# The hybrid layer and its FP4 FFN as a fourth layer of the batch flow

## The chip, the cores and the metric

The kernel runs on one core of one Trainium2 chip. The metric is the device time of one execution in microseconds, taken as the median of several runs. The engines are named TensorE (PE, and PEld for its weight loads), VectorE (DVE), ScalarE (ACT), GpSimd (POOL) and SyncE (SP), which issues DMAs. Each works through its own instructions in order and waits on semaphores for the others.

## The reference

Eight sequences of 512 tokens with 128 features pass through sixteen residual layers, `x = x + f(layernorm(x))`: four groups of attention, FFN, another attention, FFN. The last two layers are the ones that are moved, `L3_attn_b` (called the hybrid here) and `L3_ffn`; the second is also the FFN of the layer before the hybrid.

```python
def hybrid(x):                              # b, s, d = 8, 512, 128
    xn = rms(x, w_norm_in)
    route_in = xn.mean(axis=1)
    probs = softmax(silu(route_in @ router_w1) @ router_w2 + router_b2)
    p_medium, p_full = probs[:, 1], probs[:, 2]
    ssm_out = scan(state = lam * state + (1 - lam) * xn)    # over the tokens
    a1 = softmax(q1 @ k1.T / sqrt(32)); a2 = softmax(q2 @ k2.T / sqrt(32))
    slr_out = ((a1 - slr_lam * a2) @ v) @ slr_wo
    mixed = ssm_out + (p_medium + p_full) * slr_out
    mixed[:, -1] += p_full * (softmax(xn[:, -1] @ landmarks.T / sqrt(d)) @ landmarks)
    out = x + rms(concat([mixed, xn]) @ mix_w, w_norm_out)
    summary = out.mean(axis=1) @ bus_compress               # one row per sequence
    return out + 0.1 * (summary @ bus_publish) @ bus_expand

def fp4_linear(x, w):                       # blocks of 16, E2M1 grid
    return fp4_quant_dequant(x) @ fp4_quant_dequant(w).T

def ffn(x):
    return fp4_linear(silu(fp4_linear(x, w_gate)) * fp4_linear(x, w_up), w_down)
```

The `ttt` branch of the original has no effect on its output and is left out above; with a single published row per sequence its softmax is 1.

## The kernel before

All of `x` stays on the chip as eight batches (the sequences, `xb(b)`) of four tiles of 128 tokens. The first eight layers run one after the other, each with its own order, and are not touched but for where their constants lie. Then comes the flow: `stream([l2a, l2b, l3a])` takes three attention layers, each with its FP4 FFN, as 24 virtual batches `v = 8 * layer + b`. The work of a virtual batch is cut into named steps: layer norm (`st`, `sh`, `ap`), projections (`T`, `pq` ... `rv`), running maxima of the scores (`m` with group, head and unit, reduced in `f`, placed by `h` and `i`), scores and exponentials (`x`), weighting (`w`, `c`, `t`, `d`), output (`aT`, `po`, `bi`, `o0` to `o4`, `ad`), the FFN's norm, quantising and transpose (`F0` to `F8`), gates and their Silu (`V`, `S`, line 1324), up product (`U`, `y`), quantising of the hidden quarter (`z`, `D`, `C`, `A`, `M`) and the narrow product (`n`, `N`, `E`).

`in_order` issues them: the string `STREAM` is one iteration, a word `name:k` takes the step of the batch that entered k iterations ago, and there are 24 + 5 = 29 iterations, 0 to 28. Nothing is scheduled behind that: the words' order is the order on every engine. The steps of the FFN proper stand at 5, so a batch's FFN runs five iterations after its norm. PSUM is two pairs of banks (`sc`) and four single banks (`bank`), shared by all steps. In `quantize_part` the rounding of quarters 0 and 2 of the hidden tile runs on VectorE and that of quarters 1 and 3 on GpSimd.

Behind the flow, `hybrid` (line 2228) loads its weights, first norms, transposes and sums all eight batches, runs one router for the eight at once, joins the bus matrices (lines 2333 to 2339), and then runs `hybrid_batches`, a software pipeline of its own over the batches: scores of 512 by 512 for two maps (line 2387), their maxima (2391), exponentials (2396), the difference of the two maps (2411 to 2415), a product with a scaled identity that transposes it (2425), copies (2426), the weighting (2437), the mix (2459, 2460) and the norm of the output. Behind that `fp4_ffn` runs the last FFN in a pipeline of its own (lines 2151 to 2179), with the quantising of a whole hidden tile of 1408 columns at a time (lines 1984 to 2012).

```python
for i in range(B + 4):
    b1, b2, b3, b4 = (k if 0 <= k < B else None for k in (i, i - 1, i - 2, i - 3))
```

Of the kernel before, what the change touches and what calls it, by code (L numbers as in the profile page):

```python
# [22 lines left out]
F32 = mybir.dt.float32  # L23
# [6 lines left out]
P = 128  # L30
# [3 lines left out]
FF = 352  # L34
# [48 lines left out]
class Net:  # L83
    def __init__(self, ctx, tc, a):
# [12 lines left out]
        xd = a["X"].rearrange("b (t p) d -> p (b t) d", p=P)  # L97
        nc.sync.dma_start(self.xb(0), xd[:, 0:NT, :])
        self.c = g.tile([P, N_CONST], F32, name="consts")
        nc.scalar.dma_start(self.c, a["consts"])  # L100
        for b in range(1, B):
            nc.sync.dma_start(self.xb(b), xd[:, b * NT : (b + 1) * NT, :])
# [4 lines left out]

        self.maskbf = g.tile([P, 2 * P], BF16, name="maskbf")
        for k in range(2):
            nc.vector.tensor_copy(self.maskbf[:, k * P : (k + 1) * P], self.cc(C_MASK + 384, P))  # L110
# [7 lines left out]
        nc.gpsimd.memset(self.least[:, 1:2], -1e-12)  # L118

# [10 lines left out]
    def cc(self, at, n):  # L130
        return self.c[:, at : at + n]
# [440 lines left out]
    def moe(self, side=None):  # L572
# [17 lines left out]
        with self.tc.tile_pool(name="moe", bufs=2) as pool, self.tc.tile_pool(  # L590
# [35 lines left out]
            else:  # L626
# [40 lines left out]
                le, bc(at[0:1], 1, TILES), bc(self.c[0:1, C_IOTA : C_IOTA + TILES], 2, EXPERTS), ALU.is_le  # L667
# [249 lines left out]
    def max_parts(self, pool, dram, qs, ks, head, causal):  # L917
# [8 lines left out]
        def unit(g, j, u):  # L926
            if not box:
                box["nm"] = pool.tile([P, NT, 16], F32, tag="nm", name="nm", bufs=3 if causal else 2)
                if causal:
                    box["pm"] = pool.tile([P, 16, 10], F32, tag="pm", name="pm", bufs=3)  # L930
# [177 lines left out]
    def stream(self, layers):  # L1108
# [5 lines left out]
        with tile_pool(name="flow_fix", bufs=1) as fix, tile_pool(name="flow", bufs=2) as pool, tile_pool(  # L1114
# [9 lines left out]
            def layer(n):  # L1124
                key, ffn_key, rope, eps, post = layers[n]
                w = self.weights(f"{key}_w")
                rows = self.rows(f"{key}_rows")
# [4 lines left out]
                if ffn_key not in ffn:  # L1132
                    ffn[ffn_key] = self.ffn_pool.tile([P, 2 * FF + 3 * P], F32, tag="fp4_w", name="fp4_w")
                    nc.scalar.dma_start(ffn[ffn_key], self.ffn[ffn_key])
# [158 lines left out]
            def ffn_parts(v, w, rows, cols, ffn_w, rope, eps, post):  # L1293

                b, box = v % B, {}
                gu, dn = ffn_w[:, 0 : 2 * FF], ffn_w[:, 2 * FF :].rearrange("p (c n) -> p c n", c=3)
# [69 lines left out]
            def parts(v):  # L1366
                n = v // B
                if n not in made:
                    made[n] = layer(n)
                loaded[v] = [None] * 4, [None] * 4, [None] * 4  # L1370
# [7 lines left out]
            self.in_order(self.STREAM, parts, B * len(layers))  # L1378
            self.sm = outer

# [6 lines left out]
        g0 f1:3 g1 S0:5 U0:5 x101:3 m120:2 U1:5 y0:5 w0:3 z0:5 y1:5 c0:3 D0:5 m132:2 m102:2 x111:3 h1:3 aT:4  # L1387
        t0:3 z1:5 d0:3 D1:5 C0:5 V1:5 A0:5 m100:2 i1:3 M0:5 S1:5 po:4 bi:4 C1:5 o0:4 m130:2 T:1 A1:5 m020:2
        U2:5 x112:3 y2:5 o1:4 m121:2 m002:2 n0:5 x102:3 pq:1 z2:5 o2:4 rq:1 Pq:1 D2:5 M1:5 mg x110:3 Rq:1
        o3:4 m112:2 U3:5 y3:5 m101:2 N0:5 E0:5 o4:4 ad:4 z3:5 D3:5 m131:2 x200:3 x201:3 m011:2 m021:2 w1:3  # L1390
        C2:5 A2:5 M2:5 F0:4 c1:3 x202:3 l3:2 m122:2 l2:2 x211:3 pk:1 rk:1 m001:2 x210:3 m010:2 n1:5 m031:2
        m022:2 x212:3 x311:3 C3:5 m012:2 m032:2 m000:2 m110:2 sq:1 Pk:1 m030:2 t1:3 m111:2 F1:4 A3:5 d1:3
        x310:3 n2:5 f0:2 Rk:1 w2:3 M3:5 F2:4 m302:2 m321:2 m331:2 N2:5 c2:3 h0:2 i0:2 x301:3 F3:4 N1:5 E2:5
        E1:5 F4:4 x302:3 m212:2 m202:2 m300:2 n3:5 sk:1 m200:2 m301:2 x300:3 m220:2 x312:3 N3:5 E3:5 m312:2
        m330:2 t2:3 m210:2 d2:3 pv:1 m201:2 m232:2 l1:1 rv:1 F5:4 x010:2 F6:4 F7:4 x000:2 st w3:3 x012:2
        c3:3 m322:2 m221:2 x011:2 m231:2 x100:2 m211:2 F8:4 t3:3 x002:2 d3:3 m310:2 sh x001:2 m222:2 m320:2
        V0:4 m332:2 l0:1 ap m230:2 m311:2
    """
    BLOCK = """
# [1326 lines left out]
```

## Time and profile before

| | |
| --- | --- |
| median of 3 runs | 3687.51 us (3686.36 to 3687.9) |
| profiled execution, its own time | 3658.49 us |
| its span, first to last instruction | 3656.8 us |
| granted TensorE clock, mean | 0.872 |
| TensorE, VectorE busy | 2905.8, 2488.8 us (79%, 68%) |
| ScalarE, GpSimd busy | 2001.4, 1797.9 us (55%, 49%) |
| chain that ended last | TensorE 50%, VectorE 17%, GpSimd 12%, DMA 9%, ScalarE 7% |

Times in the profile are counted from the span's start. Busy shares are means over stages with different limits, so the view by stretches says more: in the windows view each row is a stretch of time, with the busy microseconds of each engine, the number of its instructions in brackets, the granted clock, the share of the DMA engines and GB/s. The waits view names who waited, for whom, microseconds in total, times, and the longest. A row of a group of instructions ends in busy time and mean nanoseconds of one, then the idle time before them. A row of the timeline begins with start and duration in microseconds.

### The profile page before, as it was taken

What the parts mean: (1) busy time and instruction counts of PE and PEld (TensorE: products, weight loads), DVE (VectorE), ACT (ScalarE), POOL (GpSimd) and SP (SyncE); (2) the same over time, 40 slices, a digit from 0 to 9 for tenths busy, and PEclk for the clock granted to TensorE, in tenths of its full rate; (3) what the DMA queues carried; (4) which work ended last, traced back from release to release, by engine and by line L of the source; (5) the groups of instructions that cost most, each with busy time, mean ns of one, the idle gap of its engine ahead of it and who ended that gap; (6) DMA issues with size and microseconds to landing.
All of it is one profiled execution on the core that took longest, in us unless ns stands there. A gap on an engine that the chain in (4) does not pass through costs nothing.

```text
span 3656.8 us, 63518 instructions
## 1 busy us (share of the span) xinstructions
PE 2905.8 (79%) x21247; PEld 1888.6 (52%) x21247; DVE 2488.8 (68%) x6913; ACT 2001.4 (55%) x3877; POOL 1797.9 (49%) x2398
## 2 busy tenths in 40 slices
PE   4757928999958747585664899999999999976867
PEld 2436912333327735483564456666665666644546
DVE  4555328888744357543453799999999999965667
ACT  3432325777732333153333477888887777754444
POOL 2223443332014466244134478767787777763345
PEclk8877958999978967687877999999999999986778
DMA  2001232222001311021014222111121121100000
GB/s 92 10 16 40 67 95 68 64 64 67 29 14 52 102 28 29 15 56 29 24 45 107 80 73 68 71 68 66 63 76 62 60 73 59 63 8 1 1 1 24
DMA packets 129655, 185.56 MB, mean 51 GB/s; under 512 B 18994, under 2 KB 98354, under 8 KB 129206
## 3 DMA queue, kind: packets, MB, share of 16 engines
q1 hardware_dynamic: 99030, 134.88, 10.9%
q0 software_dynamic: 15616, 35.47, 3.8%
q10 hardware_dynamic: 14688, 11.14, 1.0%
q8 instruction: 176, 2.88, 0.3%
q14 instruction: 145, 1.19, 0.1%
HBM read 128.96 MB, written 52.46 MB: 50 GB/s over the span
## 4 chain that ended last, share of the span: by engine, by line
PE 50%; DVE 17%; POOL 12%; DMA 9%; ACT 7%; issue 3%; SPq 1%; DVEq 0%; ACTq 0%; POOLq 0%; PEld 0%; PEldq 0%
PE av L1054 6%; DMA k<-d 6%; PE sc L733 5%; PE av L749 5%; PE sc L1023 5%; PE mx L942 5%; PE m L244 2%; DVE nm L961 2%; ACT e L1033 2%; PE sc L1308 1%; PE mx L939 1%; POOL e L1036 1%; PE m L1153 1%; PE sc L386 1%; POOL got L800 1%
## 5 line engine op out<-in xcount | busy, mean ns | idle before, releaser
L1033 ACT ACTIVATE e<-sc 128x1024 f32<-128x1024 f32 (+1 forms) x832 | 742.5, 926 | 182.2 <-PE sc L1023 136.1
L954 DVE TENSOR_REDUCE pm<-mx 128x4 f32<-128x512 f32 (+1 forms) x1152 | 625.7, 593 | 45.2 <-PE mx L942 39.6
L942 PE MATMUL mx<-k,q 126*128 126x512 bf16 (+3 forms) x2048 | 545.4, 327 | 99.4 <-DMA k<-d 87.5
L1023 PE MATMUL sc<-q,k 128*128 128x512 bf16 (+3 forms) x2048 | 446.0, 321 | 14.2 <-ACT e L1033 12.9
L1036 POOL TENSOR_SCALAR_AFFINE_SELECT e<-e 128x256 f32<-128x256 f32 x768 | 296.6, 408 | 194.4 <-ACT e L1033 190.2
L961 DVE TENSOR_REDUCE nm<-mx 128x1 f32<-128x512 f32 x512 | 324.5, 684 | 84.7 <-PE mx L942 83.7
L712 POOL DMA_INDIRECT xg<-xd,srci x220 | 210.7, 958 | 344.7 <-DVE srci L705 191.9
L1054 PE MATMUL av<-e,vaug 128*32 128x512 f32 (+3 forms) x4096 | 370.0, 482 | 2.5 <-ACT e L1033 1.8
L942 PEld LDWEIGHTS <-q 126*128 126x128 bf16 x2048 | 198.0, 99 | 307.7 <-issue 237.8
L244 PE MATMUL m<-ident,xn 128*128 128x128 f32 x480 | 108.6, 335 | 256.2 <-ACT xn L212 117.9
L1023 PEld LDWEIGHTS <-k 128*128 128x128 bf16 x2048 | 179.7, 98 | 186.7 <-issue 107.6
L939 PE MATMUL mx<-maskbf,identbf 128*128 128x128 bf16 (+1 forms) x1152 | 262.7, 238 | 15.6 <-DVE h L1333 5.3
L733 PE MATMUL sc<-xgT,w1c 128*128 128x128 f32 x1760 | 240.8, 281 | 2.5 <-DVE w1c L721 2.5
L749 PE MATMUL av<-moe_w,h 128*128 x1760 | 234.7, 277 | 1.0 <-ACT xgT L727 0.6
L800 POOL DMA_INDIRECT got<-yd,posi x192 | 192.4, 1002 | 76.4 <-issue 49.9
L733 PEld LDWEIGHTS sc<-xgT,w1c 128*128 128x128 f32 x1760 | 222.6, 198 | 2.6 <-issue 2.6
L244 PEld LDWEIGHTS m<-ident,xn 128*128 128x128 f32 x480 | 68.1, 159 | 299.6 <-ACT xn L212 135.6
L749 PEld LDWEIGHTS av<-moe_w,h 128*128 128x128 f32 x1760 | 216.2, 194 | 2.0 <-ACT xgT L727 0.7
L1054 PEld LDWEIGHTS av<-e,vaug 128*32 128x32 f32 x4096 | 108.4, 110 | 192.8 <-issue 147.4
L233 ACT ACTIVATE xn<-x,ln_shift,rstd 128x128 f32<-128x128 f32 x352 | 144.7, 485 | 103.9 <-DVE ln_shift L228 103.8
L721 DVE COPY w1c<-moe_w 128x516 f32 x220 | 100.9, 459 | 136.3 <-DVE y L758 63.2
L736 ACT ACTIVATE h<-sc 128x512 f32<-128x512 f32 x142 | 84.8, 597 | 160.5 <-PE sc L733 160.2
(461 smaller groups left out, 6434.6 us busy)
## 6 DMA issues: line engine op xcount, KB each, us to landing
q<-d SPq DMA_DIRECT2D x128, 288.0 KB
k<-d SPq DMA_DIRECT2D x384, 96.0 KB
d<-thirds SPq DMA_DIRECT2D x48, 384.0 KB
yd<-y SPq DMA_DIRECT2D x220, 64.0 KB
xd<-xn ACTq DMA_DIRECT2D x24, 256.0 KB
d<-thirds SPq DMA_DIRECT2D x48, 128.0 KB
moe_w<-in_moe_w POOLq DMA_DIRECT2D x8, 516.0 KB
moe_w<-in_moe_w POOLq DMA_DIRECT2D x8, 512.0 KB
```

What stands on the lines that cost most here:

```text
L244: nc.tensor.transpose(pt[:, t * P : (t + 1) * P], src[:, t, :], self.ident)
L733: nc.tensor.matmul(ps[:, cols], lhsT=w1c[i][:, cols], rhs=xgT[i], start=True, stop=True)
L749: nc.tensor.matmul(ps[:, 0:P], lhsT=h[i][:, c * P : (c + 1) * P], rhs=w2[:, bass.ds(e + c * P, P)], start=c == 0, stop=c == 3,)
L800: nc.gpsimd.indirect_dma_start(got[b][k][:, i, :], None, yd, bass.IndirectOffsetOnAxis(ap=posi[:, j : j + 1], axis=0))
L939: nc.tensor.matmul(out, lhsT=self.identbf, rhs=mask, start=True, stop=False, skip_group_check=True)
L942: nc.tensor.matmul(s[:, col : col + n], lhsT=q[:, t, :], rhs=key[:, 0 : n // P, :], start=not causal, stop=True, skip_group_check=True,)
L954: nc.vector.tensor_reduce(box["pm"][:, h, at : at + n // P], s[:, 0:n].rearrange("p (k n) -> p k n", n=P), AX.X, ALU.max,)
L961: nc.vector.tensor_reduce(box["nm"][:, u, h : h + 1], s, AX.X, ALU.max, negate=True)
L1023: nc.tensor.matmul(s[:, jj, col : col + n], lhsT=key[:, t, :], rhs=q[:, at // P : (at + n) // P, :], start=True, stop=True,)
L1033: nc.scalar.activation(e, s[:, :, 0:wide], AF.Exp, scale=scale)
L1036: nc.gpsimd.affine_select(out=e[:, :, col : col + P], in_=e[:, :, col : col + P], pattern=[[0, 2], [1, P]], compare_op=ALU.is_ge, fill=0.0 ...
L1054: nc.tensor.matmul(acc[g][32 * j : 32 * j + 32, at : at + n], lhsT=vaug[:, t, first : first + 32], rhs=pair[j // 2][:, j % 2, col : col + ...
```

## The change

The hybrid becomes the fourth entry of the flow, `("l3b", "l3f", None, None, None)`, and `hybrid`, `hybrid_layer`, `hybrid_batches` and `fp4_ffn` are taken out. Its work is cut into steps `H` (norm, transpose, router, landmarks), `I` (queries, values, averages, scan), `K` with a tile (scores, maxima, exponentials, difference, transposing product, copy) and `J` (weighting, mix, norm, output, bus), with `st`, `sh`, `ap` in front and the flow's own FFN steps behind. The router runs for each batch by itself. The copies of the transposed weights are written in halves. `in_order` leaves one empty place (24) in front of the hybrid's batches, which take places 25 to 32. The weights of the hybrid take the slot of the first FP4 weights and are loaded by ScalarE's queue when the layer is first asked for, at the first word of iteration 25.

`STREAM` has 58 new words and its old words in a somewhat different order; `m320`, `m322` and `m311` go from 2 to 3. The tiles `nm` and `pm` have two buffers instead of three. The constants of the first layers move to a pool that ends before the flow, loaded in two pieces, with the rotary tables, which stay, as a third. Lines of code that are only moved or renamed are left out below, and of the hybrid's steps only some are shown.

```diff
+        nc, a = self.nc, self.a
+        xd = a["X"].rearrange("b (t p) d -> p (b t) d", p=P)
+        nc.sync.dma_start(self.xb(0), xd[:, 0:NT, :])
+        self.c = pool.tile([P, N_CONST - 2 * S], F32, name="consts")
+        nc.scalar.dma_start(self.c[:, 0:C_COS], a["consts"][:, 0:C_COS])
+        nc.scalar.dma_start(self.c[:, C_COS:], a["consts"][:, C_RSEL:])
+        for b in range(1, B):
+            nc.sync.dma_start(self.xb(b), xd[:, b * NT : (b + 1) * NT, :])
+        nc.scalar.dma_start(self.rotary, a["consts"][:, C_COS:C_RSEL])
...
+        if C_COS <= at < C_RSEL:
+            return self.rotary[:, at - C_COS : at - C_COS + n]
+        at -= 2 * S if at >= C_RSEL else 0
...
-                box["nm"] = pool.tile([P, NT, 16], F32, tag="nm", name="nm", bufs=3 if causal else 2)
+                box["nm"] = pool.tile([P, NT, 16], F32, tag="nm", name="nm")
                 if causal:
-                    box["pm"] = pool.tile([P, 16, 10], F32, tag="pm", name="pm", bufs=3)
+                    box["pm"] = pool.tile([P, 16, 10], F32, tag="pm", name="pm")
...
-                w = self.weights(f"{key}_w")
-                rows = self.rows(f"{key}_rows")
...
-                    ffn[ffn_key] = self.ffn_pool.tile([P, 2 * FF + 3 * P], F32, tag="fp4_w", name="fp4_w")
-                    nc.scalar.dma_start(ffn[ffn_key], self.ffn[ffn_key])
+                    ffn[ffn_key] = self.ffn_pool.tile([P, 1188], F32, tag="fp4_w", name="fp4_w")
+                    nc.scalar.dma_start(ffn[ffn_key][:, 0 : 2 * FF + 3 * P], self.ffn[ffn_key])
+                if rope is None:
+                    return self.hybrid_weights(fix), self.rows("l3b_rows"), None, ffn[ffn_key], rope, eps, post
+                w = self.weights(f"{key}_w")
+                rows = self.rows(f"{key}_rows")
...
+                if layers[n][2] is None:
+                    out = self.hybrid_parts(pool, v % B, *made[n][0:2])
+                    out.update(ffn_parts(v, *made[n]))
+                    return out
...
+            late = B * [x[2] for x in layers].index(None) if None in [x[2] for x in layers] else None
+            self.in_order(self.STREAM, parts, B * len(layers), late)
...
+    def hybrid_weights(self, fix):
+        nc, a = self.nc, self.a
+        w = self.ffn_pool.tile([P, 1188], F32, tag="fp4_w", name="l3b_w")
+        nc.scalar.dma_start(w, a["l3b_w"])
+        lam = w[:, 928:929]
+        keep = fix.tile([P, 1], F32, tag="keep", name="keep")
+        nc.vector.tensor_scalar(keep, lam, -1.0, 1.0, ALU.mult, ALU.add)
+        bus = w[:, 736:864]
+        for part in (w[:, 608:736], w[:, 480:608]):
+            ps = self.bank("m")
+            nc.tensor.transpose(ps[:, 0:P], part, self.ident)
+            turned = fix.tile([P, P], F32, tag="turned", name="turned")
+            nc.scalar.copy(turned, ps[:, 0:P])
+            ps = self.bank("m")
+            nc.tensor.matmul(ps[:, 0:P], lhsT=turned, rhs=bus, start=True, stop=True)
+            bus = fix.tile([P, P], F32, tag="bus", name="bus", bufs=1)
+            nc.vector.tensor_copy(bus, ps[:, 0:P])
+        return w, keep, bus
...
+        def hidden():
+            hid = box["hid"] = small(1, "hhid")
+            nc.scalar.activation(hid[0:64], box["r"][0:64, 0:1], AF.Silu, scale=1.0 / S)
...
+        def exponentials():
+            t = box["lg"]
+            nc.scalar.activation(t[0:1, 0:3], t[0:1, 0:3], AF.Exp, bias=t[0:1, 4:5], accum_out=t[0:1, 5:6])
+            t = box["at"]
+            nc.scalar.activation(
+                t[0:1, 0:64], t[0:1, 0:64], AF.Exp, bias=t[0:1, 64:65], scale=D**-0.5, accum_out=t[0:1, 65:66]
+            )
...
+        def scores(t):
+            s = tiles["s", t] = self.sc()
+            for k in range(2):
+                r = slice(32 * k, 32 * k + 32)
+                nc.tensor.matmul(
+                    s[:, k, :], lhsT=box["q"][r, t * P : (t + 1) * P], rhs=box["k"][r, :], start=True, stop=True
+                )
...
+        def maxima(t):
+            nm = tiles["nm", t] = self.small([P, 2], "df_nm")
+            nc.vector.tensor_reduce(nm, tiles["s", t], AX.X, ALU.max, negate=True)
+            nc.vector.tensor_scalar(nm, nm, scale, None, ALU.mult)
...
+        def exps(t):
+            s, nm = tiles.pop(("s", t)), tiles.pop(("nm", t))
+            tot = tiles["tot", t] = self.small([P, 2], "df_tot")
+            e = tiles["e", t] = pool.tile([P, 2, S], F32, tag="e512", name="e", bufs=6)
+            for k in range(2):
+                nc.scalar.activation(
+                    e[:, k, :], s[:, k, :], AF.Exp, bias=nm[:, k : k + 1], scale=scale, accum_out=tot[:, k : k + 1]
+                )
...
+        def differ(t):
+            e, tot = tiles["e", t], tiles.pop(("tot", t))
+            inv = self.small([P, 2], "df_inv")
+            nc.vector.reciprocal(inv, tot)
+            nc.vector.scalar_tensor_tensor(inv[:, 1:2], inv[:, 1:2], rows[:, 259:260], tot[:, 0:1], ALU.mult, ALU.mult)
+            over = tiles["over", t] = small(P, "hover")
+            nc.gpsimd.tensor_scalar(over, self.ident, inv[:, 0:1], None, ALU.mult)
+            nc.vector.scalar_tensor_tensor(e[:, 1, :], e[:, 1, :], inv[:, 1:2], e[:, 0, :], ALU.mult, ALU.subtract)
+        def turn(t):
+            e, over = tiles.pop(("e", t)), tiles.pop(("over", t))
+            pt = tiles["pt", t] = self.bank("m")
+            for k in range(NT):
+                kk = slice(k * P, (k + 1) * P)
+                nc.tensor.matmul(pt[:, kk], lhsT=e[:, 1, kk], rhs=over, start=True, stop=True)
+        def turned(t):
+            if t == 0:
+                box["AT"] = [pool.tile([P, 2, S], F32, tag="e512", name="AT", bufs=6) for _ in range(2)]
+            pt = tiles.pop(("pt", t)).rearrange("p (k q) -> p k q", k=NT)
+            for i, part in enumerate(box["AT"]):
+                nc.scalar.activation(
+                    part[:, :, t * P : (t + 1) * P], pt[:, 2 * i : 2 * i + 2, :], AF.Copy, scale=-1.0
+                )
...
+        parts = {"st": stats, "sh": shift, "ap": apply}
+        names = "abcdefghijklmnopq"
+        first = (first_squares, first_norm, turn_x, sum_tokens, route, hidden, at_landmarks, logits, biased)
+        first += (exponentials, shares, spread, gates, recall, recalled)
+        parts.update({f"H{n}": f for n, f in zip(names, first)})
+        second = (queries, keep_queries, value_products, values, averages, scan)
+        parts.update({f"I{n}": f for n, f in zip(names, second)})
+        last = (weigh, context, project_out, gated, mix, last_squares, last_norm, residual, sums, keep_sums, add)
+        last += (publish, published)
+        parts.update({f"J{n}": f for n, f in zip(names, last)})
+        for n, f in zip(names, (scores, maxima, exps, differ, turn, turned)):
+            parts.update({f"K{n}{t}": lambda f=f, t=t: f(t) for t in range(NT)})
+        return parts
...
+        g0 m320:3 S0:5 Hn:3 m322:3 x101:3 m112:2 U0:5 Ke1:3 Jg:4 m311:3 Hj:2 Ho:3 Jh:4 f1:3 Id:2 y0:5 m120:2
+        Jk:4 w0:3 z0:5 U1:5 y1:5 D0:5 c0:3 aT:4 x111:3 h1:3 z1:5 Kc3:3 Hk:2 t0:3 C0:5 g1 d0:3 i1:3 Kd3:3
+        V1:5 Ke2:3 A0:5 S1:5 D1:5 m130:2 Ka0:2 M0:5 m102:2 po:4 bi:4 m132:2 T:1 Kf1:3 C1:5 o0:4 m121:2 A1:5
+        Ji:4 x112:3 Kb0:2 m020:2 U2:5 pq:1 o1:4 Jj:4 Kf2:3 y2:5 n0:5 z2:5 rq:1 mg x102:3 m002:2 D2:5 x110:3
+        Jl:4 o2:4 m110:2 M1:5 Jm:4 U3:5 l2:2 y3:5 m100:2 Pq:1 N0:5 Kc0:2 z3:5 o3:4 Ka2:2 o4:4 Kd0:2 ad:4
+        x201:3 Ke3:3 E0:5 m031:2 m011:2 Ka1:2 Ke0:2 x200:3 Rq:1 D3:5 m101:2 w1:3 C2:5 c1:3 A2:5 M2:5 x202:3
+        F0:4 l3:2 Kf3:3 Ha:1 x210:3 m032:2 Kf0:2 Ja:3 Hl:2 Kb2:2 C3:5 m012:2 m131:2 Jb:3 pk:1 rk:1 x211:3
+        m021:2 n1:5 m030:2 m010:2 x212:3 sq:1 m122:2 x311:3 m022:2 m111:2 A3:5 t1:3 Pk:1 d1:3 M3:5 m001:2
+        Hm:2 m000:2 n2:5 Rk:1 x310:3 F1:4 f0:2 w2:3 m302:2 m321:2 Jc:3 m331:2 N2:5 Kb1:2 Jd:3 F2:4 h0:2 c2:3
+        i0:2 x301:3 x302:3 N1:5 E2:5 F3:4 E1:5 If:2 Kc2:2 m330:2 m301:2 Kc1:2 Je:3 n3:5 F4:4 m200:2 Hb:1
+        m201:2 sk:1 Kd1:2 x312:3 m210:2 t2:3 N3:5 E3:5 Jf:3 Hc:1 d2:3 Hd:1 Ka3:2 l1:1 m300:2 x300:3 m202:2
+        pv:1 F5:4 m220:2 He:1 Hf:1 m312:2 Ia:1 F6:4 F7:4 Ie:1 x010:2 rv:1 st x000:2 m222:2 w3:3 x012:2 c3:3
+        Hg:1 m232:2 Ib:1 m221:2 x100:2 Ic:1 x011:2 Kb3:2 m212:2 t3:3 d3:3 F8:4 sh l0:1 Hh:1 Kd2:2 m310:2
+        x002:2 m230:2 x001:2 m211:2 m332:2 V0:4 Hi:1 m231:2 ap
     """
...
+    def in_order(self, order, parts, n=B, late=None):
...
+        gap = late is not None
+        for i in range(n + gap + max(k for _, k in order)):
             for name, k in order:
                 b = i - k
+                if gap and b >= late:
+                    b = b - 1 if b > late else n
...
-            self.hybrid,
-            lambda: self.fp4_ffn("l3f"),
+            ("l3b", "l3f", None, None, None),
+            None,
...
-                flow = range(max(first, 8), min(upto, 14), 2)
+                flow = range(max(first, 8), upto, 2)
                 if flow:
                     self.stream([layers[n] for n in flow])
-                    self.back = None
-                with tile_pool(name="turned2", bufs=1) as pool:
-                    if upto > 14:
-                        self.xT = pool.tile([P, B * S], F32, name="xT")
-                    for n in range(max(first, 14), upto):
-                        layers[n]()
```

## The prediction

> **What bounds the kernel now.** I read the page's 40 slices first, to see which stretches leave engines free, then the busy times by stage. In the slices the share of VectorE and the granted clock are high from slice 24 to 35 and fall behind it: the last fifth of the flow and the two stages after it are not full.
>
> ```profile
> PE   4757928999958747585664899999999999976867
> DVE  4555328888744357543453799999999999965667
> ...
> PEclk8877958999978967687877999999999999986778
> ```
>
> The second view is the windows table. Its cuts are the opening of an iteration of the flow (the gates' Silu, line 1324) for iterations 5, 24, 25, 26, 27 and 28, then the flow's end, the end of the hybrid's preparation, the end of its batch loop, and the end.
>
> ```profile
> core 0: us, PE busy (x) PEld busy (x) DVE busy (x) ACT busy (x) POOL busy (x), PEclk, DMA share, GB/s
> ...
> 2139.30:3118.10 978.80, 945.23 (x7874) 601.56 (x7873) 905.87 (x2524) 786.68 (x1273) 739.94 (x1166) 1.00 0.19 67
> ...
> 3215.10:3253.80 38.70, 32.22 (x268) 19.34 (x266) 21.97 (x77) 29.46 (x49) 27.22 (x46) 0.97 0.05 18
> 3253.80:3285.50 31.70, 19.10 (x74) 13.14 (x74) 16.87 (x60) 10.17 (x22) 17.86 (x21) 0.72 0.00 0
> 3285.50:3304.50 19.00, 12.28 (x48) 8.28 (x47) 9.89 (x34) 5.39 (x14) 12.10 (x14) 0.73 0.01 2
> 3304.50:3340.00 35.50, 15.18 (x50) 9.15 (x51) 19.47 (x72) 16.98 (x80) 12.78 (x19) 0.52 0.00 0
> 3340.00:3530.00 190.00, 158.81 (x750) 98.51 (x748) 115.32 (x258) 88.68 (x263) 65.17 (x77) 0.79 0.00 1
> 3530.00:3656.80 126.80, 92.82 (x452) 67.91 (x450) 99.40 (x182) 55.81 (x106) 64.33 (x42) 0.83 0.06 17
> ```
>
> To be seen: a full iteration (19 of them in the first row, 51.5 us each) is TensorE's, 945.2 of 978.8 us or 97%. From the flow's end to the end are 352.3 us, 44 us a batch, in which TensorE is busy for 76%, VectorE 66%, ScalarE 46%, GpSimd 40%. Third, the waits of those 352 us (waiter, releaser, us in total, times, longest):
>
> ```profile
> POOL over L2414 <- DVE df_inv L2411: 69.2, 18, 5.1
> ACT e L2396 <- DVE df_nm L2392: 43.7, 14, 4.5
> ...
> POOL rms_rs L171 <- ACT junk L2466: 35.4, 8, 6.9
> POOL h L2012 <- DVE qh_a L2009: 32.3, 8, 4.9
> ```
>
> One engine waits for the next inside a batch. So nothing but a chain of small steps, with too little beside it, holds this stretch; work of the other stage could lie there.
>
> **The change, part by part.** The hybrid's eight batches take the places 25 to 32 of the flow (24 stays empty), so the flow runs 32+1+5 = 38 iterations, not 29, and both stages behind it go. What an iteration then holds decides. The work of one batch of hybrid plus FP4, from the last three rows by eight:
> VectorE (19.47+115.32+99.40)/8 = 29.3 us. The router per batch adds some 13 instructions at about 0.15 us, 2.0; the layer norm's scaling goes to ScalarE (four at 0.35, less 1.4); two of four quarters of the rounding go to GpSimd (4.7 to 3.5, less 1.2). Sum 28.7.
> ScalarE (16.98+88.68+55.81)/8 = 20.2; the scaling, four at 0.49, 2.0; the weights' copy in halves, eight at 0.37 for four at 0.59, 0.6; the router's three functions, 1.2; the FP4's copies in smaller pieces, 0.8; and four table loads, since Silu (S0, S1, the router's hidden) and Exp (the router, the scores) now alternate in an iteration. A load has a row in a full iteration:
>
> ```profile
> L1324 ACT ACT_TABLE_LOAD x2 | 2.6, 1283 | 0.0
> ```
>
> Four at 1.28 are 5.1 us, beside the two loads that both old stages hold in all. Sum 29.9.
> The trace shows a load at 30.50 us, 1.28 long, and the function behind it at 31.79: nothing but the load is paid.
> The Trainium skill (ScalarE: Activation LUTs, What ACT_TABLE_LOAD costs) speaks against this change here: every switch of set costs a drain besides the load, 2.66 us in all. By it four switches are 10.6 us, ScalarE would need 35.4 us a batch and the sum below would rise by some 6 us in each of seven full iterations, 42 us, more than the whole gain; the trace's own rows do not show the drain, and I go by them.
> TensorE (15.18+158.81+92.82)/8 = 33.4 us, but at clocks of 0.52, 0.79 and 0.83; times the clock it is 26.3. Idle gaps and the clock go together in the rows (0.97 at 83% busy, 0.72 at 60%, 1.00 at 97%), so 26 to 31.
> GpSimd (12.78+65.17+64.33)/8 = 17.8, and 5.9 for the two quarters, 23.7.
> So an iteration with both cannot be under 30 us, and is not over the 44 of one after the other unless the order itself stalls. Three engines lie within 4 us of each other. Rows for how full the busiest gets: 97% in the flow, 84% (158.8/190) and 78% (99.4/126.8) in the two old loops. I take 81%, near these loops since it's their chains that run: 30/0.81 = 37 us; both ends, 31 and 44, stay for the range.
>
> Now from the opening of iteration 24 (3118.1), old and new. Old: 3656.8-3118.1 = 538.7. New:
> it 24: 49.7, as before.
> it 25: 47.3, plus the hybrid's weights. The first word of the order builds the layer: ScalarE's queue issues 594 KB and VectorE (keep), TensorE (two transposes) and ScalarE (two copies) stand right behind it in their orders.
>
> ```profile
> 3249.51 0.37 SPq L2235 DMA_DIRECT2D l3b_w<-in_l3b_w  x1
> ...
> 3254.53 0.48 DVE L2250 TENSOR_SCALAR lamT<-lamT,l3b_w 128x512 f32<-128x512 f32 x1
> ```
>
> From issue to first use 5.0 us, hidden so far by the drain; then transposes and products, 3336.6 to 3339.9, 3.3 us. All three engines queue attention work behind it. Between 0 (the engines arrive late) and 11 (nothing hidden) I take 7: 54.3.
> it 26: 38.7 with room (VectorE 22 of 38.7); a first batch's norm and projections, some 5 us on VectorE and 6 on ScalarE: 40.
> it 27: 31.7, held by the chain of batch 23 through its projection, norm and quantising, VectorE 17; about 15 us of hybrid work fit in: 34.
> it 28: hybrid without its last step, FP4 of 23: 34.
> it 29: no FP4, hybrid alone plus its quantising, VectorE and ScalarE about 25: 28.
> it 30 to 32: 3 x 37 = 111.
> it 33, 34, 35 and 36: one more step missing each time, 36, 34, 30, and 28 (the last batch's output chain and quantising in a row). it 37: the FP4 alone, 19.0 as the old last one. Store 3.5, as now (3653.3 to 3656.8).
> Sum 49.7+54.3+40+34+34+28+111+36+34+30+28+19+3.5 = 501.5, a gain of 37.2 us.
>
> The first 25 iterations get a new order too. Of its 179 old words only three change their iteration (m320, m322 and m311, one later); of the rest most stand within 0.05 of an iteration of where they stood, and some m units move by up to 0.3. The running maxima nm and pm lose a third buffer: a batch's first unit (m112:2) and the last reader of the one before (f1:3) still share two. TensorE has 3% to gain and the same work; I put 0 there, between -0.5 and +2.5 us an iteration (5% of 51.5, the idle shares of VectorE in that row being 7%). At the start the constants come in three pieces; the first normalised tile waits for GpSimd's rstd at 17.5 us behind its memsets, so 0, within 3 us either way. The l2a rows' load moves from 1.7 us to the flow's start, a whole iteration ahead of its reader: 0.
>
> The profiled execution took 3658.5 (span 3656.8), so it would take 3621.3. The median of the timed runs, 3687.5, stands 29.0 above it; carried over, 3650.
>
> **The rivals.**
> Tight overlap, chance 0.15. The full iterations run at 31 to 32 us, 97% as in the first row. Some seven iterations' worth at 5.5 us less: 38 more, 3612. For it speaks that FP4 and hybrid chains are independent; against it, both old loops stay at 78 to 84%.
> No overlap, 0.20. The in-order queues string the two chains up, 41 to 44 us: 7 x 4 = 28 back, 3678, and at 44 the gain is gone but for the preparation. For it: four PSUM banks serve every product, maximum and rounding, and the output of the mix holds one across the end of an iteration; against it, the same four carry the full flow at 97%.
> Slower, 0.18. The price sits in the iterations without hybrid: the maxima's units, TensorE and VectorE in turn, were placed where VectorE had room, and the new words moved them. At 2.5 us in each of 25 iterations it is 62 us more, 25 us net, 3713. It decides from 37/25 = 1.5 us an iteration on. For it: TensorE has no slack there; against it: most words keep their neighbours.
> As summed, 0.47: 3635 to 3668.
>
> **How the numbers follow.** The likeliest case gives 3650. Two in ten may be left out: the range goes from 3612, the tight case's middle, to 3698, half-way into the slower one. About 0.2% (7 us) is what a measurement here can tell from none. Faster: 0.47+0.15 and half of the no-overlap case, 0.72. Same: 0.08 of that case. Slower: 0.18+0.02 = 0.20.
>
> **What would show it.** Openings of iterations 5 to 24 still about 51.5 us apart; a gap of some 7 us on three engines at the opening of iteration 25; 37 us between openings 30 to 33 with VectorE and ScalarE near 80% and a clock over 0.83; four table loads in each. Wrong, if the first 24 openings lie over 53 us apart, if the late ones lie over 42, or if a table load is followed by a gap.

## The result, and the profile after

| | before | after | ratio, 95% interval |
| --- | --- | --- | --- |
| first chip, 12 runs each | 3687.70 us | 3688.73 us | 0.9996 (0.9982 to 1.0011) |
| chip of e5 to e8 below, 17 and 12 runs | 3659.28 us | 3660.47 us | 0.9998 (0.9989 to 1.0007) |

No change, where 37 us less was forecast. The profiled execution of after took 3678.17 us, of which some 25 are not the change's: it opened iteration 5 at 2166.0 us, while all other profiled executions, of both kernels, did so between 2135 and 2142. The 12 timed runs of before on the first chip also lie 28 us above those on the other chips (3687.7 and 3657 to 3660, medians), so the 25 us seem to go with that chip, not with the change. For stretches ahead of the flow I therefore use a second profile of after (e5, opening at 2141.3).

The slices of after's page (busy tenths, granted clock), to be set against the three rows shown of before:

```profile
PE   5757928999958747585655799999999999998886
DVE  4555328888744357633443689999888899877984
...
PEclk8877958999978967787878899999999999997997
```

VectorE, which stood at 5 to 7 in the last five slices, is there at 7, 7, 9, 8 and 4: the tail is filled, as the change says. So where did the gain go? The windows of after, cut at the openings of iterations 5, 24, 25, 26, 27, 28, 30 to 34 (line 1337 is now the gates' Silu; 28 and 29 are one row, since 29 has no FP4):

```profile
core 0: us, PE busy (x) PEld busy (x) DVE busy (x) ACT busy (x) POOL busy (x), PEclk, DMA share, GB/s
2165.98:3155.80 989.82, 946.12 (x7872) 601.55 (x7871) 892.48 (x2488) 783.96 (x1272) 734.13 (x1159) 1.00 0.18 65
...
3155.80:3215.14 59.34, 51.83 (x417) 33.10 (x418) 45.35 (x120) 39.01 (x62) 35.67 (x57) 0.95 0.21 74
3215.14:3265.81 50.67, 49.38 (x411) 30.89 (x413) 45.73 (x126) 37.47 (x60) 30.00 (x53) 0.96 0.08 30
3265.81:3307.69 41.88, 35.44 (x278) 21.44 (x277) 22.82 (x80) 33.91 (x64) 29.41 (x47) 0.92 0.01 2
3307.69:3345.56 37.87, 29.59 (x117) 18.48 (x115) 31.06 (x88) 23.80 (x60) 23.58 (x27) 0.68 0.00 1
3345.56:3412.67 67.11, 57.87 (x269) 37.24 (x269) 51.11 (x151) 45.69 (x134) 34.66 (x42) 0.78 0.00 1
3412.67:3448.20 35.53, 29.14 (x167) 19.17 (x168) 32.90 (x100) 28.04 (x80) 26.97 (x31) 0.99 0.03 8
3448.20:3483.51 35.31, 28.71 (x167) 18.68 (x166) 32.89 (x101) 28.05 (x80) 26.96 (x31) 1.00 0.03 9
3483.51:3519.59 36.08, 30.19 (x167) 19.60 (x166) 32.87 (x100) 28.26 (x79) 26.93 (x31) 0.95 0.03 8
3519.59:3558.48 38.89, 34.14 (x165) 21.94 (x164) 32.36 (x94) 26.61 (x76) 27.85 (x31) 0.81 0.03 8
```

Three things are to be seen. The first row took 978.8 us before and takes 989.8 now, with the same TensorE work (946 us): TensorE waits for 43.7 us of it instead of 33.6. The row that ends with the opening of iteration 25 took 49.7 and takes 59.3. And the rows of iterations 27 to 29 run at clocks of 0.68 and 0.78. The full iterations, the heart of the forecast, are as forecast and a little better: 35.3 to 36.1 us, not 37.

For the first row, the waits (waiter, releaser, us in total, times, longest), before and then after, iterations 5 to 23:

```profile
PE mx L942 <- DMA k<-d: 2.2, 4, 1.7
...
DVE pm L954 <- PE mx L942: 11.0, 31, 1.5
```

```profile
PE mx L953 <- DMA k<-d: 16.8, 21, 1.8
...
PE sc L1034 <- ACT e L1044: 5.5, 15, 0.6
...
DVE pm L965 <- PE mx L953: 49.9, 116, 1.4
```

TensorE waits for the load of a key tile once in nearly every iteration, and VectorE's running maxima wait behind it. In the timeline of after, a maxima product with such a wait (1.26 us) opens at 2218.56, 0.3 us after the iteration's opening; the loads of the keys of its group had been issued from 2210.9 to 2212.4. The new order had put `m112:2` third among the maxima units of an iteration, at its opening; the old order begins that group with `m120:2`, behind `x101` and `f1`.

For the second, the timeline at the end of iteration 24 (start, duration; the bracket is the idle time before it):

```profile
3203.05 0.33 ACTq L1403 DMA_DIRECT2D l3b_w<-in_l3b_w  x1
...
3211.44 0.15 DVE L1406 TENSOR_SCALAR keep<-l3b_w 128x1 f32<-128x1 f32 x1 [5.54 <-DMA l3b_w<-in_l3b_w]
...
3211.55 0.45 PE L1411 MATMUL m<-ident,l3b_w 128*128 128x128 f32 x1 [6.38 <-DMA l3b_w<-in_l3b_w]
3212.03 0.27 ACT L1413 COPY turned<-m 128x128 f32<-128x128 f32 x1 [7.78 <-PE m L1411]
```

The hybrid's weights are used 8.4 us after their issue and three engines stand still for it.

### The profile page after: what moved, and what is told of

Read it like the earlier page. It is cut to its first block, busy times and chain, and to the rows that moved or that the text cites. A ratio compares the mean times of both kernels' runs of the same rounds, so it can differ in the third digit from the quotient of the medians.

```text
span 3676.3 us, 64102 instructions
## 1 busy us (share of the span) xinstructions
PE 2920.8 (79%) x21332; PEld 1897.3 (52%) x21332; DVE 2503.5 (68%) x7103; ACT 2061.9 (56%) x4054; POOL 1857.4 (51%) x2494
## 4 chain that ended last, share of the span: by engine, by line
PE 37%; DVE 19%; POOL 15%; DMA 13%; ACT 8%; issue 4%; SPq 2%; another core or an unknown queue 0%; DVEq 0%; ACTq 0%; POOLq 0%
DMA k<-d 9%; PE sc L744 5%; PE av L760 5%; PE av L1065 4%; PE mx L953 3%; PE sc L1034 3%; POOL e L1047 2%; DVE nm L972 2%; ACT e L1044 2%; PE m L255 2%; DMA d<-thirds 2%; SPq L926 2%; POOL left L911 1%; PE up L1321 1%; POOL got L811 1%
## 5 line engine op out<-in xcount | busy, mean ns | idle before, releaser
L1034 PE MATMUL sc<-q,k 128*128 128x512 bf16 (+3 forms) x2048 | 446.3, 322 | 20.4 <-ACT e L1044 18.8
L244 ACT ACTIVATE xn<-x,ln_shift,rstd 128x128 f32<-128x128 f32 x416 | 171.9, 495 | 111.3 <-DVE ln_shift L239 97.2
```

The source lines that it names most:

```text
L1034: nc.tensor.matmul(s[:, jj, col : col + n], lhsT=key[:, t, :], rhs=q[:, at // P : (at + n) // P, :], start=True, stop=True,)
```

## The experiments

Ratios are to the kernel before on the same chip; e1 to e4 ran on one chip, e5 to e8 on a second, e9 to e11 on a third. "Openings 5 to 24" is the time from the opening of iteration 5 to that of 24, "the rest" from there to the end.

**e1, the kernel before again**, no edit.

> The kernel before, unchanged, profiled a second time. Theory A (the profiled execution of before, 3658.5 us, was a short one of its kind, since its own timed runs are 3682 and more): the second profile lies between 3670 and 3690 us, and the extra time lies in the mixture-of-experts stages ahead of the flow of batches, where the kernel after stood 25 us later at the opening of iteration 5. Theory B (the change itself made the stages ahead of the flow 25 us longer, through the constants that it moves): the second profile shows iteration 5 opening at 2141 us again, within 3 us.

3662.7 us, the median of its chip 3660.2. Iteration 5 opens at 2141.2, openings 5 to 24 take 979.0, the rest 540.8, each within 3.4 us of the first profile. Of theory A the longer stages did not come; theory B's reading of the 25 us falls with e3, e4 and e5, kernels with the moved constants that open iteration 5 at 2140.8, 2140.8 and 2141.3. The 25 us stand in the one profile that was taken on the first chip; no profile of before was as long, so where before's 28 us lie there is not shown. The moved constants cost nothing that shows.

**e2, only the new order, in the kernel before.**

```diff
-         g0 f1:3 g1 S0:5 U0:5 x101:3 m120:2 U1:5 y0:5 w0:3 z0:5 y1:5 c0:3 D0:5 m132:2 m102:2 x111:3 h1:3 aT:4
...
+         g0 m320:3 S0:5 m322:3 x101:3 m112:2 U0:5 m311:3 f1:3 y0:5 m120:2 w0:3 z0:5 U1:5 y1:5 D0:5
...
```

> The kernel before, with only the new order of the words that it already had: no hybrid parts in the flow, no moved constants. Theory A (the new order of the attention steps costs the iterations that hold a full attention layer, +0.58 us each over iterations 5 to 23 in the two profiles): slower by 8 to 16 us, a ratio of 1.002 to 1.004, with openings 5 to 24 adding up to about 990 us instead of 979. Rival (the order costs nothing, and the 11 us of the profiles are the spread from execution to execution): within 3 us of before, openings 5 to 24 at 976 to 982 us.

Ratio 1.0049 (1.0031 to 1.0067): 18 us slower by the order of the words alone, a little more than theory A's 8 to 16. The profiles of e1 and e2 differ by 13 us: openings 5 to 24 take 988.7 us, 9.7 more than in e1, the rest 543.5, 2.7 more. The rival is out.

**e3, the old order below iteration 24, in the kernel after.**

```diff
-             for name, k in order:
+             for name, k in first if i < 24 else order:
```

`first` is the old order, and no step runs twice where the two meet.

> The kernel after, with the old order of the words in the iterations below 24 and the new order from 24 on. Theory A (the order cost ate 11 us of the gain): 3678 us, a ratio of 0.997 to before, openings 5 to 24 adding up to about 979 us. Rival (order free): the time of the kernel after, 3686 to 3690 us.

Ratio 0.9936 (0.9920 to 0.9953), 25 us under before; more than expected. Its stretch, in the windows view:

```profile
2140.82:3111.98 971.16, 941.29 (x7871) 600.47 (x7870) 902.74 (x2484) 786.10 (x1273) 733.63 (x1159) 1.00 0.19 67
```

That is 18.7 us under after's 989.8, and also 7.8 under before's 979. So the 11 us that the first comparison of openings showed was a difference of two terms: the order, about 19 us, and a gain of 8. The gain is in the rows of iterations 19 and 21 to 23, 2 us each. In 21 to 23 of before, and no longer in e3, a transposition of the flow itself waits:

```profile
3006.64 0.63 PE L244 MATMUL m<-ident,xn 128*128 128x128 f32 x4 [1.81 <-POOL rstd L169]
```

Beside it lies the preparation of the first hybrid batches (the norm at line 2271). Its code stands behind the flow, but in a part without a hand-written order (that begins again at line 2340), and its norms came to lie inside the flow: VectorE takes the statistics of twelve tiles in such an iteration and not of eight. Iteration 22 of before, e3 and e2, groups of instructions:

```profile
L187 DVE BATCH_NORM_STATS2 bnst<-x 128x6 f32<-128x128 f32 x12 | 3.2, 265 | 0.0
...
L198 DVE BATCH_NORM_STATS2 bnst<-x 128x6 f32<-128x128 f32 x8 | 2.1, 265 | 0.0
...
L187 DVE BATCH_NORM_STATS2 bnst<-x 128x6 f32<-128x128 f32 x12 | 3.2, 265 | 0.0
```

The two terms are not independent. e2, the last line, holds the same norms as before, and yet its iterations 21 to 23 take 52.4, 51.6 and 51.6 us, for 52.8, 53.3 and 53.4 in before and 51.1, 51.6 and 51.5 in e5. Under the new order the preparation costs about 1 us in iteration 21 and nothing that shows in 22 and 23. So the new order costs 9.7 us in these iterations of the kernel before (e2 against e1), and 18.7 to 20.4 in those of the kernel after (e3 against after and e5). What made iteration 19 shorter I have not traced.

That the tiles `nm` and `pm` lost a third buffer is no rival for the order's cost: iterations 5 to 12 take 399.5 us in e3, with two buffers, and 398.4 in e1, with three, both in the old order; in the new one 411.7 (e5) and 408.7 (e2), so at most 0.1 and 0.4 us an iteration.

**e4, the hybrid's weights loaded in iteration 22**, on SyncE's queue.

```diff
+                if v == 22 and len(layers) == 4:
+                    self.early_w = self.ffn_pool.tile([P, 1188], F32, tag="fp4_w", name="l3b_w")
+                    nc.sync.dma_start(self.early_w, a["l3b_w"])
...
-        w = self.ffn_pool.tile([P, 1188], F32, tag="fp4_w", name="l3b_w")
-        nc.scalar.dma_start(w, a["l3b_w"])
+        w = self.early_w
```

> The kernel after, with the hybrid layer's weights (l3b_w) loaded on SyncE's queue in iteration 22 instead of on ScalarE's queue at the moment they are needed in iteration 25. Theory A (three engines stand still for about 9.6 us on that load and the chain of small operations behind it; the load is 8.4 us of it): 6 to 8 us faster than the kernel after, 3681 us, and the multiplication by ident that reads l3b_w waits for nothing from a DMA. Rival (the stall only takes time in which ScalarE would wait for the empty place of iteration 24 to pass): within 2 us of the kernel after.

Ratio 0.9960 (0.9946 to 0.9975), 15 us under before. Iterations 24 and 25 take 52.2 and 48.1 us, together 9.7 less than in after, somewhat more than theory A's 6 to 8, and the first use waits for no load:

```profile
3183.25 0.14 PEld L1413 LDWEIGHTS m<-ident,l3b_w 128*128 128x128 f32 x1
3183.30 0.28 PE L1413 MATMUL m<-ident,l3b_w 128*128 128x128 f32 x1
```

**e5, the kernel after again**, no edit.

> The kernel after, unchanged, on the chip of the next three, so that each is set against it. Theory (its flow gains 20 us behind the opening of iteration 24 and loses 11 before it, nothing ahead of the flow): a ratio of 0.997 to 0.998 to the kernel before, the opening of iteration 5 within 3 us of 2141 us where the execution is like the other four profiled, openings 5 to 24 adding up to 990 us. Rival (no gain at all, as the first comparison had it): a ratio of 0.999 to 1.001.

Ratio 0.9998, the rival's side. Openings 5 to 24 take 991.5 us, the rest 525.6. Set against e1 that is 12.6 lost and 15.2 gained, 2.6 net, and the span is 2.5 us shorter (3658.5 and 3661.0): too little for the runs to tell.

**e6, one word of the order moved back**, in the kernel after.

```diff
-        g0 m320:3 S0:5 Hn:3 m322:3 x101:3 m112:2 U0:5 Ke1:3 Jg:4 m311:3 Hj:2 Ho:3 Jh:4 f1:3 Id:2 y0:5 m120:2
+        g0 m320:3 S0:5 Hn:3 m322:3 x101:3 U0:5 Ke1:3 Jg:4 m311:3 Hj:2 Ho:3 Jh:4 f1:3 Id:2 y0:5 m120:2
...
-        V1:5 Ke2:3 A0:5 S1:5 D1:5 m130:2 Ka0:2 M0:5 m102:2 po:4 bi:4 m132:2 T:1 Kf1:3 C1:5 o0:4 m121:2 A1:5
+        V1:5 Ke2:3 A0:5 S1:5 D1:5 m130:2 Ka0:2 M0:5 m102:2 m112:2 po:4 bi:4 m132:2 T:1 Kf1:3 C1:5 o0:4 m121:2 A1:5
```

> The kernel after with one word moved: the maxima unit m112:2, which the new order runs at the opening of an iteration, stands behind m102:2 as in the old order's neighbourhood, some 10 us later. Theory A (the new order costs 19 us in iterations 5 to 23 mainly because m112 is the first reader of a key tile whose load is issued only some 6 us before the opening: TensorE waits 16.8 us in all for that load there, against 2.2 before): 8 to 14 us faster than the kernel after, openings 5 to 24 at 976 to 982 us, and the wait of TensorE on k<-d under 6 us. Rival (the cost is spread over the many moved units; the wait of VectorE's pm for mx, 49.9 us against 11.0, stands behind all of them): under 4 us faster, openings 5 to 24 at 986 us or more.

Ratio 0.9950 (0.9937 to 0.9963), 18 us less than after on the same chip, and openings 5 to 24 take 978.3 us, 13 less. The two waits, iterations 5 to 23 of e6:

```profile
PE mx L953 <- DMA k<-d: 1.1, 3, 0.8
...
DVE pm L965 <- PE mx L953: 34.9, 95, 0.8
```

The wait for the load is gone (16.8 in after, 18.0 in e5, now 1.1). Of the 20.4 us between e5 and e3 this one word is 13; the 7 that remain (978.3 to 971.2) are spread, and the pm row, still three times that of before, goes with them.

**e7, both repairs**: the edit of e4, and that of e3 with one iteration more.

```diff
-             for name, k in order:
+             for name, k in first if i < 25 else order:
```

> Both repairs together: the old order of the words in the iterations below 25 and the hybrid's weights loaded on SyncE's queue in iteration 22. Theory (the costs are separate and add): 19 us from the order and 10 from the weights, 29 us under the kernel after, a ratio of 0.990 to the kernel before, iteration 24 at 50 and iteration 25 at 47 to 48 us. Rival (the late iterations take part of it back as a colder TensorE): 15 to 20 us under the kernel after.

Ratio 0.9888 (0.9871 to 0.9905), 42 us under after on the same chip, and faster than both kernels. Openings 5 to 24 take 973.7, iterations 24 and 25 take 52.0 and 47.4, the rest 502.1. The costs add: the ratios of e3 and e4, multiplied, are 0.9896, and openings 5 to 24 and iterations 24 and 25 give back 17.8 and 9.7 us against e5, 27.5 for the 29 of the theory. The time fell by 42 us, 13 more than the theory's. Between the spans of e5 and e7 lie 47.5 us; besides these two terms there are 6.1 from ahead of the flow, and 13.6 from iterations 28 and 29, whose steps neither edit touches.

**Clock.** The same steps of iterations 28 and 29 took 60.9 to 74.7 us in six profiles of five kernels. The windows row of e5 and that of e7:

```profile
3320.08:3394.68 74.60, 67.45 (x269) 43.12 (x269) 51.03 (x151) 46.05 (x133) 34.73 (x42) 0.66 0.00 1
```

```profile
3288.06:3349.01 60.95, 50.94 (x267) 32.85 (x267) 52.39 (x154) 45.71 (x133) 36.41 (x43) 0.89 0.00 1
```

TensorE's busy time multiplied by its clock is 44.5 and 45.3: the same work at another clock. In order of the clock, 0.66, 0.66, 0.78, 0.81, 0.89, 0.89 (e5, e6, after, e4, e3, e7) the stretch took 74.6, 74.7, 67.1, 66.3, 60.9, 61.0 us. After and e5 are one kernel, so 7.5 us of it can lie between two executions. Still, the two with the old order ahead of the late iterations (e3, e7) are the two at 0.89, so part of e7's 13.6 may follow from the order after all; one profile of each doesn't settle it. Rows of 4 us inside e5's iteration 27 show how it falls:

```profile
3298.00:3302.00 4.00, 1.92 (x15) 1.47 (x13) 3.88 (x9) 2.91 (x9) 3.63 (x6) 1.00 0.01 4
3302.00:3306.00 4.00, 0.34 (x2) 0.35 (x3) 3.93 (x9) 1.94 (x6) 3.84 (x4) 0.68 0.01 2
3306.00:3310.00 4.00, 3.48 (x15) 2.72 (x15) 2.41 (x6) 0.92 (x3) 1.30 (x2) 0.50 0.00 0
...
3318.00:3322.00 4.00, 4.00 (x9) 2.19 (x8) 0.38 (x3) 2.72 (x5) 0.00 (x0) 0.50 0.00 0
```

A wait of 5.2 us for GpSimd (`h`, line 2382) comes first, then 16 us at half clock, although TensorE is busy for 86% to 100% of them.

**e8, the first norm's scaling on GpSimd**, in the kernel after.

```diff
-            scaled(box["xr"], xn, "rs", rows[:, 0:P])
+            xr = box["xr"]
+            nc.gpsimd.tensor_tensor(xr, xn, bc(box.pop("rs"), 2, D), ALU.mult)
+            nc.gpsimd.tensor_tensor(xr, xr, bc(rows[:, 0:P], 1, NT), ALU.mult)
```

> The kernel after, with the scaling of the hybrid's first norm (xr, four operations of 2.4 us together on VectorE in a full iteration) done by GpSimd in two operations of 512 elements a row, about 1.3 us each. Theory A (the full iterations 29 to 32 are VectorE's, 32.9 us busy of 35.5, 93%): 1.5 to 2.4 us less in each of iterations 29 to 33, 8 to 12 us in all, with VectorE at 30.5 us an iteration. Rival (the chain sets the pace and VectorE only happens to be nearly full): no change within 2 us, or slower by up to 5 us as the norm's chain gets longer.

Ratio 1.0071 (1.0058 to 1.0084): slower by 27 us against after, beyond what either side expected. A full iteration of it:

```profile
3403.67:3445.38 41.71, 35.12 (x167) 22.87 (x167) 31.86 (x95) 28.16 (x79) 29.91 (x34) 0.79 0.02 7
```

VectorE gave back 1.0 us, not 2.4 (other operations of it, `e` among them, took longer), the norm's chain got longer, and TensorE's clock, 0.95 to 1.00 in after, went down to 0.79 in iterations 30, 31 and 32. GpSimd's two operations took 1.5 and 1.3 us. A nearly full VectorE was not the bound by itself; how the 27 us divide between the longer chain and the clock, this run doesn't tell.

**e9, e10: products in TensorE's waits**, on top of both repairs. `warm(out, n)` issues n bf16 products that nobody reads.

```diff
                     pt = self.bank("m")
+                    warm(pt[:, 3 * P : 4 * P], 6)
                     for c, (at, r) in enumerate(CH):
...
                     o = box["o", t] = self.bank("av")
+                    warm(o[:, 2 * P : 4 * P], 3)
```

They are issued for `v >= 22` in e9; in e10 for `v in (22, 23)`, with 16 and 8 in place of 6 and 3.

> The kernel with both repairs (early weights, old order below iteration 25), and extra bf16 products that nobody reads, written to unused columns of the banks that the last FP4 steps hold anyway: six of 128 columns before a tile's transposes, three of 256 before its narrow products, for the batches from place 22 on. They stand in TensorE's queue where it waits for GpSimd's rounded tile or ScalarE's copy. Theory A (the late iterations run over because idle TensorE loses its clock, 0.66 to 0.89 in iterations 28 and 29, and the cold stretches then last 20 us and more): clock over 0.9 in iterations 27 to 36, iterations 27 to 29 at 90 to 95 us instead of 98.8, 33 to 36 a microsecond shorter each, 6 to 12 us faster than with the repairs alone. Rival (the clock only follows the pace that the chain sets, and the products are in the way): the same time or up to 10 us slower, since they cost about 3 us of TensorE a batch.

> The same, for the batches of places 22 and 23 alone, whose FP4 steps lie in iterations 26 to 28, and more of them: sixteen of 128 columns before the transposes, eight of 256 before the narrow products of a tile. Theory A (clock): no row of 0.50 in iteration 27, 27 to 29 at 90 to 95 us instead of 98.8, the later ones as with the repairs alone; 4 to 8 us faster. Rival (in the way): about 2 to 3 us of products a tile, eight tiles, 5 to 15 us slower.

Ratios 0.9880 (0.9863 to 0.9896) and 0.9888 (0.9871 to 0.9904), not to be told from e7's 0.9888 on another chip. The profiles say more. Iteration 27 of e9:

```profile
3250.17:3285.95 35.78, 29.55 (x158) 19.97 (x157) 30.55 (x90) 23.75 (x60) 23.71 (x27) 0.86 0.00 1
```

The clock there rises from 0.66 (e7) to 0.86, and to 0.95 in e10, and the iteration gets 2 us shorter (37.8 to 35.8 and 35.9), though TensorE has more to do. That fits the clock as a cause there, but does not show it: in the kernels without extra products iteration 27 took 37.0 us at 0.62 (e4) and 37.9 at 0.74 (e5), the colder one less. But iterations 28 and 29 take 61.3 us at 0.88 in e9 and 71.4 at 0.78 in e10: the products did not hold the clock there, and e10's dearer products lie in that stretch as well. Of theory A the clock of iteration 27 holds; that of 28 and 29 doesn't. e9 has the lowest median of all, 3609.9 us beside 3656.5 for before.

**e11, two tiles rounded by VectorE**, on top of both repairs.

```diff
-                    box["q", t] = self.quantize_part(pool, h, FF, "qh", 2, t in (1, 3))
+                    box["q", t] = self.quantize_part(pool, h, FF, "qh", 2, t in (1, 3) and v not in (22, 23))
```

> The kernel with both repairs, and the rounding of tiles 1 and 3 of the batches in places 22 and 23 done by VectorE instead of GpSimd (two operations of about 0.5 us for three of about 0.95). Theory A (TensorE's wait of 6.9 us in all for GpSimd's h in iterations 27 to 29, the longest 2.6 to 5.2, is what lets the clock fall): that wait under 3 us, 27 to 29 at 92 to 95 us instead of 98.8, 4 to 7 us faster. Rival (VectorE, 81 to 86% busy in these iterations, is what the tile would wait for instead): within 2 us.

Ratio 0.9888 (0.9872 to 0.9905), iterations 27 to 29 at 37.4 and 61.5 us and a clock of 0.61 in 27: the rival's time. TensorE's wait for `h` fell from 6.9 us (e7) to 2.5, so taking most of that one wait away does not keep the clock up.

## Why the prediction was wrong

The mechanism was right: the stage's chain was the bound, work of the other stage fits into it, and the rest went from 540.8 to 525.6 us. The sum was wrong in the following steps, with e1 and e5.

**The new order, put at 0 "between -0.5 and +2.5 us an iteration": this step failed.** It cost 18.7 to 20.4 us over iterations 5 to 23 (e3 against after and e5), 1.0 us in each. Alone in the kernel before (e2) it cost 9.7 us there, and 18 in the time. The prediction saw that "most words keep their neighbours" and looked for the cost in the maxima's VectorE room. It did not follow the word that now opens a group back to its load: `m112:2`, first reader of keys whose DMA is issued 6 to 8 us earlier (e6: 13 of the 20.4). Of the old words this one had moved farthest, from 32% to 3% of the way through an iteration's words, the "up to 0.3" of the prediction. The rival with a slower end named the maxima's units as its place, with a price of 2.5 us; the place was right, and its price per iteration in fact 1.0, below the 1.5 at which it would have turned the sign. None of the prediction's signs of being wrong came: openings 52.1 to 52.2 us apart on average for 53, late ones 35.3 to 38.9 for 42, no gap behind a table load. They were too wide to see a loss that took most of the gain.

**The rest, 501.5 forecast, 525.6 measured in e5.** The difference of 24 by its terms (the forecast counts from the table load in front of the opening, 1.3 us earlier, in 538.7 and 501.5 alike): iterations 24 and 25 with the weights 109.1 for 104.0 (the stall is 9.7 by e4, not 7); iteration 27 37.9 for 34, by a cause that is not shown; 28 and 29 74.6 for 62, which goes with the clock (61 where it was granted 0.89); 30 to 32 107.0 for 111, the one term that was better; 33 38.9 for 36, at a clock of 0.81; 36 and 37 with the store 53.2 for 50.5; the others within 1 us. The prediction had the rows of 0.72 and 0.52 before it, and used the clock to convert TensorE's work, but let the mixed iterations 27 to 29 run as if it were granted there.

**What it left out, in its favour:** 8 us, the hybrid's norms and whatever else iterations 19 and 21 to 23 held before. It took the whole preparation to lie behind the flow, as the code's order has it. The 8 us hold beside an order cost of 20.4; with the 9.7 of e2 for the order, the other parts of the change cost 2.8 us in these iterations (988.7 to 991.5) and saved nothing. Either way some 12.6 us are lost there.

**Engine sums in a full iteration.** ScalarE 28.0 for 29.9, GpSimd 27.0 for 23.7, VectorE 32.9 for 28.7. VectorE, not ScalarE, is the fullest, at 93%. The router is not what was missed (13 operations of 2.1 us together, for 2.0). The norms' statistics are: 3.6 us an iteration, for 1.9 a batch in the three rows that the sum started from, because the hybrid's lay in the flow; its scaling, for which 1.4 was taken off, stood in these rows with 0.2. The scaling `xr` took twice as long an operation, after in iterations 30 to 32 beside before behind its flow:

```profile
L1448 DVE SCALAR_TENSOR_TENSOR xr<-xn,rms_rs,l3b_rows 128x128 f32<-128x128 f32 x12 | 7.2, 655 | 0.0
...
L2266 DVE SCALAR_TENSOR_TENSOR xr<-xn,rms_rs,l3b_rows 128x128 f32<-128x128 f32 x32 | 9.3, 346 | 5.7 <-POOL rms_rs L173 5.7
```

The FP4's maxima, reciprocals and residual in smaller pieces took some 2 us more. So the forecast of 37 us was near by luck: two errors, the work and the 81%, cancelled.

The loads of function tables came as forecast, four a batch, with nothing behind them (ScalarE's timeline of a full iteration):

```profile
3417.49 1.28 ACT L1337 ACT_TABLE_LOAD   x1
3418.79 0.76 ACT L1337 ACTIVATE sg<-sc 128x704 f32<-128x704 f32 x1
```

The Trainium skill (ScalarE: Activation LUTs, What ACT_TABLE_LOAD costs) has a drain of about 1.38 us with each load. The gaps in front of the loads and behind them are 0.02 and 0.01 us in these iterations, and the measurement decides: 1.28 a load here.

**Put together:** 37.2 forecast, minus 20.4 for the order, plus 7.8 for the preparation, minus 24.1 in the rest, and plus 2.1 because e1's rest is longer than the 538.7 that the sum started from: 2.6 are left, and 2.5 lie between the spans of e1 and e5. With both repairs the rest is 502.1 us for 501.5 forecast, though with errors that cancel in it: the weights' 7 are saved, 27 is dearer. The 29.0 us carried over from the profiled execution to the median were the first chip's; on the chips of e1 and e5 the profiled executions of the unchanged kernels (e1, e5) lie within 3 us of the medians, and the ratio stayed the same.

## What to carry to other kernels

When an order written by hand changes, follow each word that becomes the first reader of a load back to that load's issue, and see how many microseconds lie between; that most words keep their neighbours says nothing of that one, and one moved word cost 13 us here. A layer's weights that are asked for by its first step stop every engine that has this step in its order: issue them iterations earlier, on a queue that has room. In a stage whose TensorE is three quarters busy, price each row at the clock that the row itself shows, and look for the same instructions at two clocks before believing any difference there.

## What the runs showed of the hardware

The granted clock of one stretch differs from profile to profile with no difference in its work: 0.66 to 0.89, with 13.7 us between the longest and the shortest, in iterations 28 and 29 (0.78 and 0.66, 67.1 and 74.6 us, in two profiles of one kernel), and 0.81 against 0.97 for about 2.7 us in single full iterations of one run (e3: 38.9 beside 36.2 us). After a wait of 5 us TensorE ran at half clock for 16 us while busy for 86% to 100% of them. The Trainium skill (TensorE: Matmul & The Clock Gate, What's actually happening) has the full clock return after a busy window of some 3.4 us; in these rows it took about five times that. Why 28 and 29 stay cold in some kernels and not in others is open; extra products raised it in iteration 27 and not in those.
